# Cross-attention on one core: buffers that no store holds, a transfer moved behind x1, product 7 copied later

## The chip, the cores and the metric

The kernel runs on one core of one Trainium2 chip. The metric is the time of one execution in device microseconds. The engines are named as in the profile: PE is the matmul engine, PEld its weight loads, DVE the vector engine, ACT the scalar engine, POOL the engine GpSimd, SP the engine that issues plain transfers. All data are float32.

## The reference

For each of 8 batches, with x1 and x2 of 512 channels by 1024 positions:

```
q = einsum('bcn,dc->bnd', x1, Wq) + bq        # d = 64
k = einsum('bcn,dc->bdn', x2, Wk) + bk
v = einsum('bcn,dc->bdn', x2, Wv) + bv
attn = softmax(einsum('bnd,bdm->bnm', q, k), axis=2)
out = einsum('bcm,bnm->bcn', v, attn) + x1
```

## The kernel before

The two large products of a batch are done in two stages: Y = x2 · attn (the "y" stage), and then out = Wv · Y (the "o" stage). The bias is added at the end, since each row of attn sums to one. Each stage is split two by two and done with seven products in place of eight (the Strassen-Winograd scheme): products 1, 2, 6, 7, 5, 3, 4. The sums of operands that this takes are S1 to S4 of the left and T1 to T4 of the right operand. In the "y" stage products 1, 2, 7, 5, 3 and 4 are split once more by the same scheme from batch 1 on (`multiply_seeded`, `multiply_onto`): seven inner products of two by two matmuls, whose partial state in one PSUM tile (`chain`) is copied out by ACT between them. An inner product that adds on to `chain` must wait for the copy that comes before it. Inner products run in the order 1, 7, 6, 2, 5, 4, 3, and a dictionary `hooks` names other work that is issued after one of them.

The results of the "y" stage are blocks 11, 12, 21, 22. A PSUM pair of banks `a` collects products 1, 6, 5, 3, and a pair `c` products 2, 7, 4. States in between are copied to buffers in SBUF, each with a tag; tiles of one tag share one buffer (`bufs=1`), and a later tile waits until all use of the earlier one is over, a store to DRAM included. The tags that matter here:

- `u1`: product 1's copied state (`copy_u1`, line 332), then a part of product 5's inner sums (`eI5u`, line 434), then product 7's copied state (`copy_7`, line 534), then the result's block 11 (`evict_o`, line 605), which x1 is added to and which is stored from there.
- `u6`: the copied state of product 6, in the "y" and in the "o" stage. Block 21 of the result is made in it, in place (line 609), and is stored from there.
- `yT1`: an operand sum of the "o" stage, and inner sums of products 7 and 1 of the "y" stage.
- `y12`: a part of product 7, then the operand T3 of the "o" stage.

Softmax is done column by column of the transposed scores, in two halves h of 512 queries. The maximum over the rows is folded on DVE (line 248) and reduced over the partitions on POOL (`highest`, line 258). The sum of the exponentials of half 0 is not folded on DVE from batch 1 of the next scores on: ACT copies the first of four tiles (`copy_first`, line 621), and three transfers on POOL's queue add the others to it (`add_tile`, line 618). Each of these must have landed before the next is issued. Then DVE adds the two halves of the tile (line 252, in `total`), POOL reduces (line 263), and the reciprocal takes a way through DRAM (lines 265 to 278).

x1 is added to the result by transfers that accumulate, also on POOL's queue: `add_x1` for block 21 (line 565) and line 615 for the other blocks. `add_11` (line 171) adds a block of x2 to S3 and S2 in the same way. Stores of the result are issued by SP (line 616).

The order of work on each engine is the order in which the program issues it (`manual_schedule`); each engine and each queue works in that order. `period` issues one batch's steps: `s` is the batch, `n` the next, `nn` and `nnn` those after it. In the last part of `period` the "o" stage of `s` runs while the scores and exponentials of `n` are prepared.

Of the kernel before, what the change touches and what calls it, by code (L numbers as in the profile page):

```python
# [15 lines left out]
def kernel(  # L16
# [278 lines left out]
    def exponential(s, h, i):  # L295
        e = s.e[h][:, :, i, :]
        nc.scalar.activation(e, e, AF.Exp)  # L297
# [10 lines left out]
    def open_t(s):  # L308
        for n in ("T1", "T2"):
            s.t[n] = sb.tile([P, MH, H], F32, tag=f"e{n}", name=f"e{n}_{s.b}")  # L310
        e0, e1 = s.e[0], s.e[1]
        s.t |= {"11": e0[:, 0], "12": e1[:, 0], "21": e0[:, 1], "22": e1[:, 1]}
        s.t["T3"] = s.t["12"]
# [17 lines left out]

    def copy_u1(s, j):
        if j == 0:
            s.tmp[1] = sb.tile([P, 2, H], F32, tag="u1", name=f"uy1_{s.b}")
        nc.scalar.copy(s.tmp[1][:, j, :], s.bank["a", j])  # L335

    def sum_e(s, *ks, of=(0, 2)):
# [196 lines left out]
    def copy_7(s, j):  # L534
        if j == 0:
            s.tmp[7] = sb.tile([P, 2, H], F32, tag="u1", name=f"uy7_{s.b}")
        nc.scalar.copy(s.tmp[7][:, j, :], s.bank["c", j])
# [29 lines left out]
    def evict_o(s, k):  # L567


        bank, add = RESULT[k] if k != "11" else ("p", None)  # L570
        r, h = int(k[0]) - 1, int(k[1]) - 1

        def bias(j):
            return bv_sb[:, 2 * r + j : 2 * r + j + 1]

        if s.b == B - 1 and k == "11":
            o = s.x[:, 0:2, ts(h, H)]
            for j in range(2):
                nc.vector.scalar_tensor_tensor(
                    o[:, j, :], s.bank[bank, j], bias(j), o[:, j, :], ALU.add, ALU.add  # L580
                )
                nc.sync.dma_start(out[s.b, ts(j, P), ts(h, H)], o[:, j, :])
            return
        if s.b == B - 1 and add is None:
            for j, n, engine in (
                (0, slice(0, H), nc.sync), (1, left, nc.scalar), (1, right, nc.sync)
            ):
                o = s.x[:, 2 * r + j, ts(h, H)][:, n]
                nc.vector.scalar_tensor_tensor(
                    o, s.bank[bank, j][:, n], bias(j), o, ALU.add, ALU.add  # L590
                )
                engine.dma_start(out[s.b, ts(2 * r + j, P), ts(h, H)][:, n], o)
            return
        if s.b == B - 1:
            o = s.x[:, 2 * r : 2 * r + 2, ts(h, H)]
            for j in range(2):
                nc.vector.scalar_tensor_tensor(
                    o[:, j, :], s.bank[bank, j], bias(j), o[:, j, :], ALU.add, ALU.add
                )
            for j in range(2):  # L600
                nc.vector.tensor_tensor(o[:, j, :], o[:, j, :], s.tmp[add][:, j, :], ALU.add)
                nc.sync.dma_start(out[s.b, ts(2 * r + j, P), ts(h, H)], o[:, j, :])
            return
        if add is None:
            o = sb.tile([P, 2, H], F32, tag="u1" if k == "11" else "r", name=f"r{k}_{s.b}")
            for j in range(2):
                nc.scalar.activation(o[:, j, :], s.bank[bank, j], AF.Identity, bias=bias(j))
        else:
            o = s.tmp[add]
            for j in range(2):  # L610
                nc.vector.scalar_tensor_tensor(
                    o[:, j, :], s.bank[bank, j], bias(j), o[:, j, :], ALU.add, ALU.add
                )
        if k != "21":
            nc.gpsimd.dma_start(o, block(s, k, x1), accum_op=ALU.add)
        nc.sync.dma_start(block(s, k, out), o)

    def add_tile(s, h, i):
        nc.gpsimd.dma_start(s.mx[h], s.e[h][:, :, i, :], accum_op=ALU.add)  # L619

    def copy_first(s, h):

        s.mx[h] = sb.tile([P, 2, H], F32, tag="fold", name=f"sum_{s.b}_{h}", bufs=2)
        nc.scalar.copy(s.mx[h], s.e[h][:, :, 0, :])  # L624
# [138 lines left out]
    def period(s, n, nn, nnn):  # L763
# [32 lines left out]
        def add_exponential(i):  # L796
            exponential(n, 0, i)
            add_tile(n, 0, i)

        open_t(s)  # L800
        if n is None:
            load_x(s, x1)
        if s.b == 0:
            first(1)
            head_second(s, n)
            sum_e(s, "T1", "T2")
            total(s, 0)
            load_a(n, "11")
            first(2)
            evict_y(s, "11")  # L810
            keys(n)
            load_x(nn, x1)
            sum_t4(s)
            sums(s, 1)
            shares(s, 0)
            sum_e(s, "T3")
            load_a(n, "21", "22")
            first(6)
            scores_0()
            inner_left(s, 4, s.a["22"], "a12")  # L820
            inner_right(s, 4, s.t["T4"], "eT2")
            inner_left(s, 3, s.a["S4"], "aI3")
            shares(s, 1)
            first(5)
            inner_right(s, 3, s.t["22"], "eT1")
            for i in range(MH):
                lower(n, 0, i)
            first(7)
            copy_7(s, 0)
            copy_7(s, 1)  # L830
            complete_3 = multiply_seeded(s, 3, "r")
            complete_3()
            evict_t3(s)
            evict_y(s, "22")
            scale_y(s, "11", "T3", "22")
        else:
            complete_1 = multiply_seeded(s, 1, "y11")
            sum_e(s, "T1", "T2")
            complete_1()
            for i in range(1, MH):  # L840
                fold(s, 1, i, "sum", ALU.add)
            total(s, 1)
            invert(s, 0)
            complete_2 = multiply_seeded(
                s, 2, "y22", {5: lambda: copy_u1(s, 0), 4: lambda: copy_u1(s, 1)}
            )
            if n:
                sum_t3(s, 0)
                sum_t3(s, 2)
            complete_2()  # L850
            evict_y(s, "11")
            if n is None:
                sum_e(s, "T3")
            sum_t4(s)
            first(6)
            inner_left(s, 7, s.a["S3"], "yT4")
            if five:
                inner_left(s, 5, s.a["S1"], "i2")
                inner_right(s, 5, s.t["T1"], "y21", "u1")
            sum_a(s, "S4")  # L860
            if n:
                evict_q = scores_0()
            spread(s, 0)
            shares(s, 1)
            inner_right(s, 7, s.t["T3"], "yT1", "yT2")
            inner_left(s, 3, s.a["S4"], "aI3")
            if five:
                multiply_5(s, {6: evict_q})
            else:
                first(5)  # L870
            inner_right(s, 3, s.t["22"], "eT1")
            if n:
                lower(n, 0, 0)
            complete_7 = multiply_seeded(s, 7, "y12")
            complete_7()
            evict_y(s, "22")
            if n:
                for i in range(1, MH):
                    lower(n, 0, i)
            else:  # L880
                inner_left(s, 4, s.a["22"], "a12")
                inner_right(s, 4, s.t["T4"], "eT2")

            hooks = {7: lambda: copy_7(s, 0), 2: lambda: copy_7(s, 1)}
            if n:
                hooks |= {6: lambda: exponential(n, 0, 0), 4: lambda: exponential(n, 0, 1)}
            complete_3 = multiply_seeded(s, 3, "r", hooks)
            complete_3()
            evict_t3(s)
        if n:  # L890
            if s.b:
                load_a(n, "11")
            begin_s1(n)
            scores_and(n, 1, 2, "a", nothing)
            if s.b == 0:
                exponential(n, 0, 0)
            else:
                copy_first(n, 0)
                add_tile(n, 0, 1)
            end_s1(n)  # L900
            if nn:
                next_keys()
# [13 lines left out]
        if s.b == 0:  # L916
            hooks = {6: lambda: exponential(n, 0, 1), 5: lambda: exponential(n, 0, 2)}
        elif n:
            hooks = {6: lambda: add_exponential(2), 5: lambda: exponential(n, 0, 3)}
        multiply_4(s, hooks)  # L920
        if late and n:
            negate(n, "S3")
# [7 lines left out]
        if late and n:  # L930
            for i in range(1, MH):
                fold(n, 1, i, "max", ALU.max)
            highest(n, 1)
            add_tile(n, 0, 3)
            add_11(n, "S3")
        second(1)
        if s.b == 0:
# [14 lines left out]
        second(2)  # L952
        evict_o(s, "11")
        if n:
            if s.b == 0:
                add_tile(n, 0, 3)
            inner_left(n, 1, n.a["11"], "i2")
        second(5)
        if n:
# [58 lines left out]
```

## Time and profile before

| | us |
|---|---|
| time, median of 3 runs | 689.28 |
| lowest and highest of the 3 | 687.08, 691.88 |
| time of the profiled execution | 690.05 |
| its span, from the first to the last instruction | 688.0 |
| PE busy in it | 674.7 |
| DVE busy | 614.7 |
| ACT busy | 336.5 |
| POOL busy | 218.5 |

The span is that of one execution, and the other 2.05 us of its time lie around it. Busy times are sums over the span; an engine's idle time matters only where another engine, or the end, waits for it. DMA transfers are told by their issue and by the time until they land; POOL's queue carried 54.60 MB and the queue of SP 75.64 MB. The mean granted clock of PE was 0.998 of full speed.

### The profile page before, as it was taken

The page shows a single profiled execution, that of the slowest core. Times are in us where ns is not written, and L with a number is a line of the kernel's source. Part 1 is how long each engine was busy: PE and PEld are TensorE (multiplying, and loading weights), DVE is VectorE, ACT ScalarE, POOL GpSimd, SP SyncE. Part 2 cuts the span into 40 slices and gives each one's busy share as a digit, 9 for nine tenths or more (in the row PEclk, how much of TensorE's full clock was granted, in tenths as well). Part 3 has the DMA queues.
Part 4 walks back from the last instruction along what each step waited for, and adds up shares of the span by engine and source line. Part 5 has one row for each costly group of instructions (what it writes and reads, how often), then busy time and mean ns, then how long its engine had stood idle before and what let it go on. Part 6 is the DMA issues. An engine that isn't in the chain of part 4 may idle for free.

```text
span 688.0 us, 7199 instructions
## 1 busy us (share of the span) xinstructions
PE 674.7 (98%) x2420; PEld 399.0 (58%) x2420; DVE 614.7 (89%) x763; ACT 336.5 (49%) x564; POOL 218.5 (32%) x182
## 2 busy tenths in 40 slices
PE   9999999999999999999999999989999999999997
PEld 5333554766556665657647485463854747555763
DVE  1999998899999999999899999987989979999784
ACT  2734365456455464463743556515475356553320
POOL 0124215260265312542144421534213460264000
PEclk9999999999999999999999999999999999999999
DMA  9666659976996949979499785898747982699403
GB/s 303 262 216 238 127 216 155 241 146 206 235 228 184 248 121 285 197 189 287 107 257 226 166 253 146 199 219 200 230 82 170 243 177 63 122 163 278 111 10 113
DMA packets 50772, 131.09 MB, mean 191 GB/s; under 512 B 5552, under 2 KB 7856, under 8 KB 50736
## 3 DMA queue, kind: packets, MB, share of 16 engines
q0 software_dynamic: 22464, 54.60, 44.0%
q1 hardware_dynamic: 27984, 75.64, 30.4%
q10 hardware_dynamic: 288, 0.39, 0.2%
q8 instruction: 19, 0.31, 0.2%
q14 instruction: 17, 0.14, 0.1%
HBM read 87.30 MB, written 16.81 MB: 151 GB/s over the span
## 4 chain that ended last, share of the span: by engine, by line
PE 70%; DMA 15%; DVE 6%; issue 5%; ACT 2%; POOL 2%; SPq 0%; DVEq 0%; POOLq 0%; ACTq 0%
PE ps_ya L380 11%; PE ps_yc L442 6%; PE ps_oa L380 6%; PE ps_ya L442 6%; PE ps_s L228 5%; DMA r<-in_x_dram 5%; DMA out_dram<-r 4%; DMA sum<-e 4%; PE ps_oc L380 4%; PE ps_k L181 3%; PE ps_q L181 3%; PE ps_i4chain L442 3%; PE ps_o L400 3%; PE ps_i3chain L442 3%; PE ps_i7chain L442 2%
## 5 line engine op out<-in xcount | busy, mean ns | idle before, releaser
L380 PE MATMUL ps_ya<-eT,aS 128*128 128x512 f32 x176 | 79.5, 606 | 5.6 <-ACT uy L335 5.6
L263 POOL PARTITION_ALL_REDUCE den<-sum x16 | 52.6, 3285 | 93.0 <-DVE few L271 52.4
L258 POOL PARTITION_ALL_REDUCE top<-max x16 | 37.0, 2315 | 131.6 <-DVE max L252 75.9
L293 DVE TENSOR_TENSOR e<-e,top 128x1024 f32<-128x1024 f32 x60 | 69.9, 1218 | 0.0
L297 ACT ACTIVATE e<-e 128x1024 f32<-128x1024 f32 x60 | 61.8, 1057 | 4.6 <-DVE e L293 3.9
L619 POOL DMA_DIRECT2D sum<-e x21 | 25.4, 1208 | 115.8 <-ACT sum L624 45.5
L380 PEld LDWEIGHTS ps_ya<-eT,aS 128*128 128x128 f32 x176 | 33.6, 193 | 47.8 <-issue 38.7
L380 PE MATMUL ps_oa<-yT,w_S 128*128 128x512 f32 x128 | 57.5, 592 | 0.0
L380 PE MATMUL ps_oc<-yT,w 128*128 128x512 f32 x128 | 57.4, 592 | 0.0
L237 ACT COPY e<-ps_s 128x1024 f32<-128x1024 f32 x46 | 45.6, 1031 | 9.1 <-PE ps_s L228 8.8
L228 PE MATMUL ps_s<-q,k 64*128 64x512 f32 x188 | 47.6, 608 | 0.9 <-ACT q L646 0.8
L380 PEld LDWEIGHTS ps_oc<-yT,w 128*128 128x128 f32 x128 | 24.3, 190 | 30.6 <-issue 28.9
L380 PEld LDWEIGHTS ps_oa<-yT,w_S 128*128 128x128 f32 x128 | 24.3, 190 | 30.6 <-issue 30.6
L248 DVE TENSOR_TENSOR max<-max,e 128x1024 f32<-128x1024 f32 x30 | 36.8, 1225 | 2.2
L391 ACT COPY uo<-ps_oa 128x512 f32<-128x512 f32 x32 | 18.7, 585 | 35.0 <-PE ps_oa L380 33.9
L391 ACT COPY uy<-ps_ya 128x512 f32<-128x512 f32 x24 | 13.9, 589 | 39.1 <-PE ps_ya L380 36.8
L228 PEld LDWEIGHTS ps_s<-q,k 64*128 64x128 f32 x188 | 17.0, 186 | 24.5 <-issue 17.5
L479 ACT COPY ps_ya<-ps_i1chain 128x256 f32<-128x256 f32 x28 | 10.0, 357 | 42.2 <-PE ps_i1chain L442 38.7
L547 DVE TENSOR_TENSOR y<-y,den 128x1024 f32<-128x1024 f32 x24 | 29.3, 1221 | 0.3
L418 DVE TENSOR_TENSOR aI<-a 128x256 f32<-128x256 f32 x58 | 29.0, 541 | 0.0
L380 PE MATMUL ps_oa<-y,w_S 128*128 128x512 f32 (+1 forms) x68 | 28.8, 567 | 0.0
L400 PE MATMUL ps_o<-y,w 128*128 128x512 f32 x64 | 28.8, 592 | 0.0
(201 smaller groups left out, 1549.6 us busy)
## 6 DMA issues: line engine op xcount, KB each, us to landing
x_in_x_dram<-in_x_dram SPq DMA_DIRECT2D x60, 512.0 KB, 6.9
a<-in_x2T_dram SPq DMA_DIRECT2D x32, 512.0 KB, 9.8
sum<-e POOLq DMA_DIRECT2D x21, 512.0 KB, 6.0
aS<-in_x2T_dram POOLq DMA_DIRECT2D x14, 512.0 KB, 8.8
uo<-in_x_dram POOLq DMA_DIRECT2D x14, 512.0 KB, 10.3
r<-in_x_dram POOLq DMA_DIRECT2D x14, 512.0 KB, 12.3
out_dram<-r SPq DMA_DIRECT2D x14, 512.0 KB, 6.2
out_dram<-uo SPq DMA_DIRECT2D x14, 512.0 KB, 4.6
```

The source lines that it names most:

```text
L181: nc.tensor.matmul(ps[r, :], w_sb[:, c, :], s.x[:, c, ts(h, H)], start=(c == 0), stop=(c == CT - 1),)
L228: nc.tensor.matmul(ps[g], s.k[r, ts(i, P)], s.q[r, ts(h, H)], start=True, stop=True)
L237: nc.scalar.copy(e[:, :, i, :], whole)
L248: nc.vector.tensor_tensor(f, e[:, :, 0, :] if i == 1 else f, e[:, :, i, :], op)
L258: nc.gpsimd.partition_all_reduce(s.top[h], s.mx[h][:, 0, :], P, ReduceOp.max)
L263: nc.gpsimd.partition_all_reduce(s.den[h], s.mx[h][:, 0, :], P, ReduceOp.add)
L293: nc.vector.tensor_tensor(e, e, top, ALU.subtract)
L297: nc.scalar.activation(e, e, AF.Exp)
L380: nc.tensor.matmul(ps[:, n], left[ka][:, k, ts(j, P)], right[kb][:, k, n], start=opens and k == 0, stop=i in (2, 3, 4) and k == n_k - 1, s ...
L391: nc.scalar.copy(s.tmp[i][:, j, :], ps)
L400: nc.tensor.matmul(ps, w["11"][:, k, ts(j, P)], s.y["11"][:, k, :], start=k == 0, stop=False, skip_group_check=True)
L442: nc.tensor.matmul(ps, s.inner[i][ka][:, k, :], s.inner[i, "t"][kb][:, k, :], start=opens and k == 0, stop=z in (2, 3, 4) and k == MH // 2 ...
```

## The change

Four things are done.

1. Product 1's copied state goes to the buffer `yT1` in place of `u1`. The result's block 21 goes to `y12`; before, it was made in place in `u6`. The number of instructions is the same.
2. The third of the transfers that sum half 0 is issued after `add_11` of S3, after `add_x1` of block 21, and after x1's transfer for block 11 (in `evict_o`). In batch 0 it was there already.
3. Product 7's state is copied after the second and the fifth inner product of product 3 in place of the seventh and the second.
4. In batch 6, where there is a next batch and none after it, the copy and the first transfer of half 0's sum are issued in product 4, after its seventh inner product, and no longer before it.

```diff
     def copy_u1(s, j):
         if j == 0:
-            s.tmp[1] = sb.tile([P, 2, H], F32, tag="u1", name=f"uy1_{s.b}")
+            s.tmp[1] = sb.tile([P, 2, H], F32, tag="yT1", name=f"uy1_{s.b}")
         nc.scalar.copy(s.tmp[1][:, j, :], s.bank["a", j])
...
         else:
-            o = s.tmp[add]
+            u = s.tmp[add]
+            o = sb.tile([P, 2, H], F32, tag="y12", name=f"o{k}_{s.b}") if k == "21" else u
             for j in range(2):
                 nc.vector.scalar_tensor_tensor(
-                    o[:, j, :], s.bank[bank, j], bias(j), o[:, j, :], ALU.add, ALU.add
+                    o[:, j, :], s.bank[bank, j], bias(j), u[:, j, :], ALU.add, ALU.add
                 )
...
+        def first_sum():
+            copy_first(n, 0)
+            add_tile(n, 0, 1)
...
-            hooks = {7: lambda: copy_7(s, 0), 2: lambda: copy_7(s, 1)}
+            hooks = {2: lambda: copy_7(s, 0), 5: lambda: copy_7(s, 1)}
...
             if s.b == 0:
                 exponential(n, 0, 0)
-            else:
-                copy_first(n, 0)
-                add_tile(n, 0, 1)
+            elif nn:
+                first_sum()
             end_s1(n)
...
         elif n:
             hooks = {6: lambda: add_exponential(2), 5: lambda: exponential(n, 0, 3)}
+            if nn is None:
+                hooks[7] = first_sum
         multiply_4(s, hooks)
...
             highest(n, 1)
-            add_tile(n, 0, 3)
             add_11(n, "S3")
         second(1)
...
         evict_o(s, "11")
         if n:
-            if s.b == 0:
-                add_tile(n, 0, 3)
+            add_tile(n, 0, 3)
             inner_left(n, 1, n.a["11"], "i2")
```

## The prediction

> **What bounds the kernel now.** I read the page first, then the list of waits of the matmul engine, then the timeline around its longest wait.
>
> ```profile
> span 688.0 us, 7199 instructions
> PE 674.7 (98%) x2420; PEld 399.0 (58%) x2420; DVE 614.7 (89%) x763; ACT 336.5 (49%) x564; POOL 218.5 (32%) x182
> ```
>
> PE is busy for 674.7 of 688.0 us, so nothing that runs beside it is worth anything: only PE's own idle time, 13.3 us with head and tail, and any slow matmuls can be won. Who ends that idle time (waiter, who was waited for: us, times, longest):
>
> ```profile
> PE ps_ya L380 <- ACT uy L335: 5.6, 3, 3.8
> PE ps_i3chain L442 <- ACT ps_ya L479: 1.0, 1, 1.0
> PE ps_warm L691 <- DVE warm L688: 1.0, 1, 1.0
> PE ps_s L228 <- ACT q L646: 0.8, 1, 0.8
> PE ps_ya L380 <- ACT e L288: 0.3, 1, 0.3
> PE ps_i4third L442 <- ACT e L237: 0.3, 1, 0.3
> ```
>
> The first line is `copy_u1` (line 335): three times the matmuls of product 6 stand until product 1's state has been copied. The second is one wait in product 3. The rest is the head and 0.3 us in batch 6. The timeline tells why the copy is late (start, duration, what; in brackets the idle time before it and what ended it):
>
> ```profile
> 430.96 1.19 POOL L619 DMA_DIRECT2D sum<-e  x1 [9.07 <-ACT ps_oa L404]
> 435.36 1.89 POOL L258 PARTITION_ALL_REDUCE top<-max  x1 [3.21 <-DVE max L252]
> 441.67 1.20 POOL L619 DMA_DIRECT2D sum<-e  x1 [4.42 <-ACT e L297]
> 442.97 2.04 POOL L565 DMA_DIRECT2D uo<-in_x_dram  x1
> 443.73 2.50 POOL L615 DMA_DIRECT2D r<-in_x_dram  x1
> ...
> 450.73 0.68 DVE L252 TENSOR_TENSOR sum<-sum 128x512 f32<-128x512 f32 x1
> 453.43 1.41 DVE L611 SCALAR_TENSOR_TENSOR uo<-ps_oc,bv_sb,uo 128x512 f32<-128x512 f32 x2 [2.02 <-DMA uo<-in_x_dram]
> ...
> 455.94 0.40 SPq L616 DMA_DIRECT2D out_dram<-r  x1
> ...
> 458.40 1.23 DVE L306 TENSOR_TENSOR eT<-eT,e 128x1024 f32<-128x1024 f32 x1
> ...
> 465.34 0.58 ACT L335 COPY uy<-ps_ya 128x512 f32<-128x512 f32 x1 [4.52 <-DMA out_dram<-r]
> ...
> 465.97 8.83 PE L380 MATMUL ps_ya<-eT,aS 128*128 128x512 f32 x16 [3.83 <-ACT uy L335]
> ```
>
> The third transfer of half 0's sum (441.67) stood on POOL for the second to land, and x1 for block 11 (443.73) stood behind it. That x1 lands as SP issues the store, 455.94; the store reads buffer u1, which the copy on ACT must overwrite, so ACT waits for it until 465.34 and PE until 465.97. PE then takes 8.83 us for 16 instructions that take 7.13 us at 379.89. The windows say why (columns: us, busy time and instructions of PE, PEld, DVE, ACT, POOL, granted clock, DMA share, GB/s):
>
> ```profile
> 466.00:471.00 5.00, 5.00 (x8) 2.19 (x9) 4.63 (x11) 4.48 (x6) 4.70 (x6) 0.66 0.61 206
> ```
>
> After the 3.83 us pause the granted clock is low for some 3.4 us.
>
> **The change part by part.** *The copied state in yT1.* No instruction is added. The copy now waits for the last reader of yT1, the matmuls of product 1's own inner sums, over by 455.3 here, instead of the store. In this place the next thing to end is T2 for product 6 at 458.40+1.23 = 459.63, while PE reaches product 6 at 462.1, so no second wait stands close behind. Gone: the 5.6 us of line 335 (0.20 at 379.89, 3.83 at 465.97, 1.57 at 628.05) and 8.83-7.13 = 1.70 us of slow matmuls. The wait on the store passes to the next user of u1, DVE's line 434 for product 5's inner sums at 472.46; the store had landed by 465.3, so 7 us are to spare, and a store still later would cost DVE the excess.
>
> The Trainium skill ("TensorE: Matmul & The Clock Gate", "What's actually happening") has the clock fall only after an idle window of about 3.4 us that runs freely, so a pause like this one costs clock in some runs and none in others. The 1.57 us pause here kept a clock of 1.00, which fits. By the page the 1.70 us might be missing from a median run, and the time would be 683.4 us in place of the one below; I keep the row.
>
> *Block 21 in y12.* DVE's two additions (1.41 us for both) write another buffer. u6 is then free when they end (about 454.8) and not when the store lands. ACT's copy of product 6 waited for that store once, 2.3 us, with PE not stopped: worth nothing by itself, but without it a 2.3 us wait could show once PE runs earlier. y12's readers, the matmuls of the second stage's product 7, are over some 3 us before, and its next writer, a copy in product 7, comes more than 20 us after the store's issue (at 490 against 465.34).
>
> *The third transfer behind x1.* On POOL it passes three issues from batch 1 on: `add_11` of S3, x1 for block 21, x1 for block 11. These three no longer wait for the second transfer; around 441 they would issue from 437.25, when the top reduction ends, and x1 of block 11 land about 6 us earlier. The price is that `sum` lands last of the four. Transfers of this queue land one after the other (issue to landing 5.5 us for the first, then about 2.5 to 3 us each), so the four end about where x1 of block 11 ended before, 0.4 to 0.6 us earlier where POOL had waited. Against the start of DVE's line 252:
>
> - batches 1 to 6, old landing (the store's issue, line 616): 204.87, 287.22, 369.04, 455.94, 538.50, 616.79;
> - DVE reaches line 252 at 204.28, 286.28, 368.27, 450.73, 538.51, 616.13.
>
> That makes a new DVE wait of 0 to 0.7 us each, and about 1.2 us at 450.73 (four landings of some 2.6 us after the second's 441.1 give 451.9), where the old 2.02 us wait for x1 of block 21 goes. Behind it on DVE are block 21, T1 and T2, and product 6 waits for T2. T2 ends 2.3 to 3.7 us before PE gets there (294.03 against 297.69 in an undisturbed stretch), so PE pays nothing. Later DVE has about 0.44 us before product 7's completion and 0.75 us before product 3's. Bounds: 0 and six times 1 us; I take 0, since batch 0 has just this order already, and a longer wait:
>
> ```profile
> 123.81 0.69 DVE L252 TENSOR_TENSOR sum<-sum 128x512 f32<-128x512 f32 x1 [3.13 <-DMA sum<-e]
> 161.96 0.58 ACT L537 COPY uy<-ps_yc 128x512 f32<-128x512 f32 x1 [1.45 <-DVE y L556]
> 162.87 1.13 PE L442 MATMUL ps_i3chain<-eI3eT,aI 128*128 128x256 f32 x4 [1.04 <-ACT ps_ya L479]
> ```
>
> A wait of 3.13 us cost PE 1.04 us, 39 us later, because `copy_7` on ACT stood for DVE and the copy that frees `chain` stood behind it.
>
> *Product 7 copied later.* Both copies (0.58 us) move two inner products back, behind that copy (0.38 us) and an exponential (1.06 us). The `chain` copy comes right after its matmuls, so the 1.04 us go. What stands behind `copy_7` now is the copy for inner product 3, whose matmuls come two inner products (2 x 0.86 us) after those that waited, so the tolerance for a late DVE grows by 1.7 us. The 0.3 us of batch 6 stay; its first transfer, put off into product 4, takes a 1.09 us copy of ACT from before that product to its middle: -0.3 to +0.5, taken as 0.
>
> *Sum.* 5.6 + 1.7 + 1.04 = 8.3 us. The profiled execution took 690.05 us (688.0 of span, 2.05 around it), so 681.7 us. The median shown is 689.28 us and the lowest 687.08; I read their 4.8 us of spread as these stalls being longer or shorter, over one floor. I set no other offset.
>
> **Rivals.** *Part comes back* (20%). The pauses go, but DVE, 89% busy, becomes the bound after 466, where PE comes 5.5 us earlier. For it: DVE's idle time there is 2.02+0.53+0.91+3.03 = 6.5 us, and 1.2 us of new wait leave it level. Against it: the other stretches run level without a stop of PE. At 2 to 3 us back: 684 us. The missing clock loss ends in the same place.
>
> *The wait only moves* (6%). Something else holds ACT's copy or product 6, such as its own left operand or DVE's completion of product 1. Against it: both were through about 2 to 4 us before PE. Only the 1.04 us would go: 689 us.
>
> *Slower: the sum lands late in every batch* (7%). The place is DVE's line 252. The slack before product 6 is 3.65 us; what is above stops PE, six times. The net is a loss from 3.65+8.3/6 = 5.0 us. For it: one x1 transfer took 17.2 us to land; issued at about 275.2 that is 292.4, a wait of 6.1 us, and 681.7 + 6 x 2.45 = 696.4 us. Against it: the longest `sum` took 11.5 us, at four in a row.
>
> **How the numbers follow.** The forecast has 67%: 681.7 us, alone 680.3 to 683.5. A measurement of this kernel can tell about 1% from no change, here below 682.4 or above 696.2 us. The forecast lies close to the first bound: some 50 of its 67 fall below, and 2 of the part that comes back, so faster 0.52. Slower takes half of its rival and a little for what I overlooked: 0.06. The rest, 0.42, is within 1%. The range reaches up to the part that comes back: 680.3 to 686.5.
>
> **What would show it.** Right: no wait of PE on line 335 and none of `ps_i3chain`, a clock of 1.00 from 7 us to the end, no ACT wait on `out_dram<-r`, DVE line 252 waiting 0 to 1.5 us for `sum<-e` in batches 1 to 6, PE busy 673 us in a span near 680. Wrong: PE waits on `eT` or on lines 485 and 306, a DVE wait at line 252 above 3 us, or line 434 waiting for a store.

## The result, and the profile after

| | before | after |
|---|---|---|
| median, us | 690.28 (4 runs, 687.08 to 691.88) | 682.42 (4 runs, 681.23 to 682.56) |
| profiled execution: time, span | 690.05, 688.0 | 682.56, 680.8 |
| PE busy in it | 674.7 | 672.1 |

The ratio is 0.9888, with a 95% interval of 0.9848 to 0.9928: 1.1% faster. The forecast was 681.7 us.

From the page after:

```profile
span 680.8 us, 7209 instructions
PE 672.1 (99%) x2420; PEld 397.9 (58%) x2420; DVE 615.2 (90%) x763; ACT 336.9 (49%) x564; POOL 218.5 (32%) x182
```

PE is busy 2.6 us less with the same 2420 instructions. Most of it is one stretch that ran at half the clock before. PE's waits after (waiter, who was waited for: us, times, longest):

```profile
PE ps_warm L692 <- DVE warm L689: 1.0, 1, 1.0
PE ps_sa L228 <- DVE yT L542: 0.9, 1, 0.9
PE ps_k L181 <- DMA x_in_x_dram<-in_x_dram: 0.8, 2, 0.6
PE ps_s L228 <- ACT q L647: 0.8, 1, 0.8
PE ps_q L643 <- DMA x_head<-in_x_dram: 0.7, 1, 0.7
PE ps_ya L380 <- ACT e L288: 0.3, 1, 0.3
PE ps_i4third L442 <- ACT e L237: 0.3, 1, 0.3
```

The wait for `copy_u1` is gone, and so is the one of `ps_i3chain`. In their place stands one new wait, for line 542 (`evict_t3`), 0.9 us. The waits for `ps_k` and `ps_q` are the first loads from DRAM. The timeline around the place of the longest pause, after:

```profile
437.64 0.92 POOL L171 DMA_DIRECT2D a<-in_x2T_dram  x1
438.20 1.59 POOL L565 DMA_DIRECT2D uo<-in_x_dram  x1
438.91 2.08 POOL L616 DMA_DIRECT2D r<-in_x_dram  x1
442.42 1.18 POOL L620 DMA_DIRECT2D sum<-e  x1 [1.42 <-DMA sum<-e]
...
449.59 0.40 SPq L617 DMA_DIRECT2D out_dram<-r  x1
452.11 0.69 DVE L252 TENSOR_TENSOR sum<-sum 128x512 f32<-128x512 f32 x1 [0.77 <-DMA sum<-e]
...
458.65 1.23 DVE L306 TENSOR_TENSOR eT<-eT,e 128x1024 f32<-128x1024 f32 x1
...
461.25 0.60 ACT L335 COPY uy<-ps_ya 128x512 f32<-128x512 f32 x1
...
462.51 7.03 PE L380 MATMUL ps_ya<-eT,aS 128*128 128x512 f32 x16
```

x1 of block 11 (`r`) is issued right behind the reduction, and its store at 449.59 in place of 455.94. The third transfer is issued last of the four, and DVE waits 0.77 us for it at line 252. The copy has no idle time in front of it in brackets, and the 16 matmuls of product 6 take 7.03 us in place of 8.83. The granted clock (the column behind POOL's busy time) in the same window as before:

```profile
466.00:471.00 5.00, 5.00 (x17) 2.10 (x17) 4.86 (x11) 2.48 (x5) 4.70 (x6) 1.00 0.04 1
```

It is 1.00 where it was 0.66. PE works on 17 matmuls there, the end of product 6 and the first scores, where it was 8 of product 6 alone.

### The profile page after: what moved, and what is told of

Read it like the earlier page. It is cut to its first block, busy times and chain, and to the rows that moved or that the text cites. A ratio compares the mean times of both kernels' runs of the same rounds, so it can differ in the third digit from the quotient of the medians.

```text
span 680.8 us, 7209 instructions
## 1 busy us (share of the span) xinstructions
PE 672.1 (99%) x2420; PEld 397.9 (58%) x2420; DVE 615.2 (90%) x763; ACT 336.9 (49%) x564; POOL 218.5 (32%) x182
## 4 chain that ended last, share of the span: by engine, by line
PE 84%; DVE 6%; DMA 5%; issue 2%; ACT 1%; SPq 1%; POOL 1%; DVEq 0%; POOLq 0%; ACTq 0%
PE ps_ya L380 11%; PE ps_oa L380 11%; PE ps_yc L442 8%; PE ps_oc L380 7%; PE ps_ya L442 6%; PE ps_s L228 5%; PE ps_o L400 4%; PE ps_o L380 4%; PE ps_k L181 3%; PE ps_q L181 3%; PE ps_i4chain L442 3%; PE ps_i3chain L442 3%; PE ps_i7chain L442 2%; PE ps_i1chain L442 2%; PE ps_i2chain L442 2%
## 5 line engine op out<-in xcount | busy, mean ns | idle before, releaser
L380 PE MATMUL ps_ya<-eT,aS 128*128 128x512 f32 x176 | 77.5, 594 | 0.0
L620 POOL DMA_DIRECT2D sum<-e x21 | 32.1, 1530 | 108.7 <-ACT sum L625 42.0
```

The costliest lines, as they stand in the source:

```text
L380: nc.tensor.matmul(ps[:, n], left[ka][:, k, ts(j, P)], right[kb][:, k, n], start=opens and k == 0, stop=i in (2, 3, 4) and k == n_k - 1, s ...
```

## Experiments

Two theories for the main gain stand against each other: the copy had to leave the buffer that the store holds, or the store had to be earlier. The first two runs do one part each, on the kernel before. One measure is used throughout: PE runs the same 2420 matmuls in every version, so when the same matmul starts in two traces tells how far PE is ahead or behind at that place. An idle time can set it back by more than its own length, since the matmuls behind a pause start further apart.

**The buffers alone.**

```diff
-            s.tmp[1] = sb.tile([P, 2, H], F32, tag="u1", name=f"uy1_{s.b}")
+            s.tmp[1] = sb.tile([P, 2, H], F32, tag="yT1", name=f"uy1_{s.b}")
...
+            o = sb.tile([P, 2, H], F32, tag="y12", name=f"o{k}_{s.b}") if k == "21" else u
```

> The kernel before with the first part alone: product 1's state in yT1, block 21 in y12. My theory (the buffer held by the store is the whole cause of the three pauses): no wait of PE on line 335, granted clock 1.00 after the head, although x1 of block 11 lands as late as before (about 11 to 12 us after its issue, its store landing after product 2's end at least in one batch). No DVE wait at line 252 from batch 1 on. One PE wait of about 1.0 us in product 3 stays. Time 682 to 683 us. Rival (the transfer's place is what counts): PE still waits 2 us or more in all at product 6, for T2 or the left operand, and the time is 685 us or more.

Measured: 681.54 us (4 runs, 681.28 to 682.0) beside 689.71 before, ratio 0.989 (0.9866 to 0.9914). Its timeline:

```profile
455.50 0.40 SPq L617 DMA_DIRECT2D out_dram<-r  x1
...
460.31 0.59 ACT L335 COPY uy<-ps_ya 128x512 f32<-128x512 f32 x1
...
461.57 7.03 PE L380 MATMUL ps_ya<-eT,aS 128*128 128x512 f32 x16
```

The store is issued as late as before (455.50; it lands 9.3 us later in the trace, at 464.8), and PE is in product 6 before that. So the buffer alone takes away the whole pause. The wait of `ps_i3chain` is there with 1.0 us and DVE does not wait at line 252 from batch 1 on, both as expected; the time is 0.5 us under the expected range.

**The transfer's place alone.**

```diff
             highest(n, 1)
-            add_tile(n, 0, 3)
             add_11(n, "S3")
...
-            if s.b == 0:
-                add_tile(n, 0, 3)
+            add_tile(n, 0, 3)
```

> The kernel before with the second part alone: the third transfer of half 0's sum behind x1 of block 11, product 1's state still in u1. My theory: x1 of block 11 lands 2 us earlier in each batch and some 6 us earlier where POOL had waited, so the store is over when the copy comes, or up to 0.5 us later: PE waits on line 335 for under 1 us in all, no loss of clock, DVE waits 0.1 to 1.5 us at line 252 in each of six batches; 682.5 to 684 us. The two parts then remove the same time twice over and must not be added. Rival (only the buffer helps): pauses of 3 us or more stay, 686 us or more.

Measured: 682.26 us (681.45 to 682.68), ratio 0.9902 (0.9873 to 0.993). PE has no wait on line 335. Its timeline:

```profile
441.01 1.18 POOL L619 DMA_DIRECT2D sum<-e  x1 [1.46 <-DMA sum<-e]
...
448.23 0.40 SPq L616 DMA_DIRECT2D out_dram<-r  x1
450.75 0.69 DVE L252 TENSOR_TENSOR sum<-sum 128x512 f32<-128x512 f32 x1 [0.86 <-DMA sum<-e]
...
459.81 0.59 ACT L335 COPY uy<-ps_ya 128x512 f32<-128x512 f32 x1
...
461.06 7.03 PE L380 MATMUL ps_ya<-eT,aS 128*128 128x512 f32 x16
```

Here the copy still uses u1, but the store issued at 448.23 lands 10.0 us later, at 458.3, 1.5 us ahead of the copy. In another batch ACT still stood 0.5 us for this store, and PE did not feel it. The time is 0.2 us under the expected range. Each of the two parts removes the same pauses by itself. They must not be added, and done together the second is a reserve.

**yT1 alone, block 21 left in u6.** The first line of the diff above.

> The kernel before with product 1's state in yT1 and nothing else; block 21 stays in u6. Forecast: block 21's buffer is worth nothing by itself, so this equals the two buffers together, 681.5 us within 0.7 us, with no PE wait on line 335. Rival: without the second buffer ACT's copy of product 6 waits for the store of block 21 (2.3 us once before) and PE, which is earlier now, shows 0.5 to 2.5 us of it in front of the scores or product 5: 682.5 us or more.

Measured: 682.33 us (681.94 to 683.25), ratio 0.9906 (0.988 to 0.9932). PE waits 0.2 us for ACT's copy of product 6, once, in the last batch: that copy goes to u6 and stood 4.46 us for the store of block 21. By the starts of the same matmuls in this trace and in that of the two buffers, the wait set PE back by 0.4 us. So block 21's buffer is worth 0.4 us here, and not nothing as the forecast had it. The medians lie 0.8 us apart, just outside the 0.7 us given, and the two ranges overlap by 0.06 us; the other 0.4 us can't be told from the spread of the runs.

**The old order of product 7's copies**, in the kernel after.

```diff
-            hooks = {2: lambda: copy_7(s, 0), 5: lambda: copy_7(s, 1)}
+            hooks = {7: lambda: copy_7(s, 0), 2: lambda: copy_7(s, 1)}
```

> The changed kernel with product 7 copied after inner products 7 and 2 as before. My theory, from the profile after: DVE is late in batch 1, and PE pays about 0.9 us for that at whichever step comes to need it first; so the 0.9 us wait for line 542 goes and a wait of about 1 us in product 3 is back: same time within 0.3 us, 682.4 us. In the other batches nothing. Rival (the forecast's step: the later copies win 1.04 us): 1 us more, 683.5 us, with the wait at line 542 kept or other waits of PE in product 3 in batches 2 to 6.

Measured: 681.82 us (681.55 to 682.22). PE's waits show what came of it:

```profile
PE ps_i3chain L442 <- ACT ps_ya L479: 1.1, 1, 1.1
```

The wait for line 542 is gone, and the one in product 3 is back. Moving the copies moved PE's wait and took nothing off it. The time is 0.6 us below the forecast of this run; the two profiled spans are 1.0 us apart, and 0.8 us of that had arisen by batch 0's keys, where the first loads from DRAM are waited for.

**Batch 0's third transfer ahead of the x1 transfers.** If both waits have one cause, DVE's late start at line 252 after batch 0, an earlier landing there should remove either.

```diff
             add_tile(n, 0, 2)
+            add_tile(n, 0, 3)
             value_sums("S3", "S4")
...
-            add_tile(n, 0, 3)
+            if s.b:
+                add_tile(n, 0, 3)
```

> The changed kernel with batch 0's third transfer issued right behind the second, ahead of the x1 transfers. Theory (DVE's wait of 3.2 us at line 252 after batch 0 is what PE pays 0.9 us for in batch 1): it lands some 5.5 us after the second, DVE waits under 0.5 us there, PE waits neither for line 542 nor in product 3 of batch 1: 0.9 to 1.4 us less, 681.2 us. Rival (DVE is late in batch 1 by its own work): PE's 0.9 us stay, 682.4 us.

Measured: 680.71 us (679.8 to 680.96), ratio 0.9878 (0.9852 to 0.9904). PE's waits in full:

```profile
PE ps_warm L692 <- DVE warm L689: 1.0, 1, 1.0
PE ps_s L228 <- ACT q L647: 0.8, 1, 0.8
PE ps_ya L380 <- ACT e L288: 0.3, 1, 0.3
PE ps_i4third L442 <- ACT e L237: 0.3, 1, 0.3
```

DVE does not wait at line 252 after batch 0, and between the head and batch 6 PE waits for nothing. That shows the cause of the 0.9 us. By the starts of the same matmuls in both traces, PE was 1.3 us ahead of the kernel after by the end of batch 0's keys (the first loads, which vary from run to run), and gained 1.4 us more in batch 1. So the wait of 0.9 us cost more than the idle time that the list shows.

**The same two kernels once more, on one chip.**

> The changed kernel again, on one chip with the version that follows it. Theory (its head varies with the first loads by 1 us or so, the rest is fixed): 681.5 to 682.5 us, PE's wait for line 542 in batch 1 of about 0.9 us again, clock 1.00, no wait on line 335. Rival (the 0.9 us were chance): no such wait, 681 us.

> The changed kernel with batch 0's third transfer right behind the second, again. Theory: PE does not wait for line 542; 1.2 us less than the changed kernel beside it (680.5 to 681.2 us). Rival (the 680.7 us of the first run were a fast head alone): within 0.4 us of the changed kernel.

Measured: the changed kernel 682.24 us (6 runs, 681.13 to 682.76), with a PE wait of 0.8 us for line 542 again; the version with batch 0's transfer early 680.47 us (5 runs, 680.07 to 680.85), without it. The two ranges do not meet. The medians lie 1.8 us apart where 1.2 was expected. In this pair of traces the changed kernel is 0.1 us ahead behind the first loads, and falls 1.4 us back in batch 1; nothing else differs by 0.1 us. Against the kernel before (688.62 there) the ratios are 0.991 (0.989 to 0.9929) and 0.9885 (0.9867 to 0.9903). This version beats both kernels.

**yT1 and batch 0's early transfer on the kernel before, nothing else.**

> The kernel before with product 1's state in yT1 and batch 0's third transfer right behind the second: the two edits that should be enough. Theory: no PE wait on line 335, none in product 3 of batch 1, no loss of clock: PE waits only in the head and 0.3 us in batch 6, 680.5 us, 1.0 us less than the buffers alone and 1 to 2 less than the changed kernel. Rival (the copies of product 7 or the other edits are needed too): 682 us or more.

Measured: 681.74 us (681.11 to 682.37), ratio 0.9898 (0.9868 to 0.9929). PE has no wait on line 335 and none in product 3, as expected, but the time missed by 1.2 us. A wait of 0.3 us for ACT at the scores of batch 1 is new, and 0.1 us for the copy of product 6 in the last batch shows. Both go back to one buffer:

```profile
139.71 1.07 ACT L391 COPY uy<-ps_ya 128x512 f32<-128x512 f32 x2 [4.10 <-DMA out_dram<-uo]
141.75 1.13 PE L228 MATMUL ps_s<-q,k 64*128 64x512 f32 x4 [0.31 <-ACT e L237]
625.60 1.14 ACT L391 COPY uy<-ps_ya 128x512 f32<-128x512 f32 x2 [4.43 <-DMA out_dram<-uo]
```

Line 391 copies product 6 to u6, which the store of block 21 still holds. ACT stood for that store four times, 10.9 us in all, and never in the runs that move block 21 to y12. By the starts of the same matmuls, against the trace with batch 0's transfer early (680.37 us), the two waits set PE back by 0.6 and 0.4 us, and product 4 of batch 6, without the transfer put off, by 0.1 us. That is about the miss. The worth of the two edits in this kernel is read from the traces; they were not added to it one by one.

**The transfer later still**: the kernel after, with the third transfer of batches 1 to 6 behind the addition to S2, so that DVE waits for it longer.

```diff
-            add_tile(n, 0, 3)
+            if s.b == 0:
+                add_tile(n, 0, 3)
...
             add_11(n, "S2")
+            if s.b:
+                add_tile(n, 0, 3)
```

> The changed kernel with the third transfer moved one place further in batches 1 to 6, behind the addition to S2. This puts a number on the slack that made the moved transfer free. It should land some 6 us after DVE could begin line 252 (in the profile after, the addition to S2 lands at 208.8 and the next transfer of this queue some 2.6 us later, against 205.1). By the slack of 3.65 us from the prediction PE waits for T2 about 2.7 us in each of six batches: 682.4 + 16 = 698 to 699 us. With a second payment in product 3 or at the scores, as batch 1 shows for a late DVE (0.9 us), 704 us. Rival (DVE's delay is absorbed elsewhere, or there is no such slack): no more than 2 us lost in all, under 685 us; or the whole 6 us are paid each time, 718 us.

Measured: 697.65 us (697.14 to 698.27), ratio 1.0127 (1.0101 to 1.0153). The size is close to the expected one, but by luck: DVE waited only 3.4 to 5.4 us at line 252 where some 6 were expected, and by the slack of 3.65 us those six waits would have cost 5.8 us in all, not 15.2. PE's longest waits:

```profile
PE ps_sa L228 <- DVE yT L542: 5.7, 5, 1.3
PE ps_i2chain L442 <- ACT ps_yc L479: 1.8, 1, 1.8
PE ps_s L228 <- ACT e L237: 1.1, 4, 0.3
```

There is no wait for T2 among them. The timeline of batch 2:

```profile
293.41 0.69 DVE L252 TENSOR_TENSOR sum<-sum 128x512 f32<-128x512 f32 x1 [4.75 <-DMA sum<-e]
...
299.83 7.03 PE L380 MATMUL ps_ya<-eT,aS 128*128 128x512 f32 x16
...
336.04 1.29 DVE L542 TENSOR_TENSOR yT<-ps_ya,uy 128x512 f32<-128x512 f32 x2
...
336.78 1.29 PE L228 MATMUL ps_sa<-q,k 64*128 64x512 f32 x3 [1.26 <-DVE yT L542]
```

DVE stands 4.75 us at 293.41, and PE starts product 6 at 299.83 on time. It pays 43 us later, when the scores of half 1 need the pair of banks `a` that line 542 has still to read. That is also where the kernel after pays its 0.9 us. PE's idle time, span less busy time, is 7.7 us longer than after, half of the 15.4 us between the spans; the other half stands as busy time, 679.8 us in place of 672.1, with the clock at 1.00. Each pause of 1.26 us at these scores set PE back by 2.1 us.

**The kernel before, profiled once more.**

> The kernel before, profiled once more. My theory (its spread of 4.8 us is the length of the pauses over one floor): PE's waits on line 335 and the loss of clock differ from those of the first profile, and the span less these is the same within 0.7 us: 688.0 - 5.6 - 1.7 = 680.7 us. Rival (the spread is elsewhere): the same pauses with another span, or a remainder off by 1.5 us or more.

Measured: 690.40 us, span 688.4. PE waits 5.3 us on line 335, 3.5 of them in one pause, again before product 6 at 466, and the granted clock falls again:

```profile
466.00:472.00 6.00, 5.62 (x9) 2.41 (x10) 5.23 (x12) 5.08 (x8) 5.70 (x7) 0.72 0.61 203
```

With about 1.8 us for the clock the remainder is 688.4 - 5.3 - 1.8 = 681.3 us, against 688.0 - 5.6 - 1.8 = 680.6 us in the first profile: within the 0.7 us expected, and both close to the span after. The before runs spread over 686.34 to 691.44 us on one chip, those after over 681.13 to 682.76. So most of the spread goes away with the pauses. But the two profiles of before have nearly the same pauses and lie in the upper part of the range, so they say little on the spread, and no timeline shows what a run near 687 us did. The mean granted clock of the runs tells more: of 27 runs of the kernel before for which it is on record, the five below 687.3 us had 1.000, and the others, all above 688.1, had 0.994 to 0.998 (the profiled execution, with its one stretch at half clock, 0.998). A mean clock of 0.994 over 688 us is a loss of some (1 - 0.994) x 688 = 4.1 us, an estimate. By it the spread is for the most part lost clock, and less the length of the pauses, as the prediction had read it. The five kept their clock and still took 4 to 5 us longer than the runs after; presumably they paused too, but that was not seen.

## Why the prediction was right, and where it was not

- **The pauses** (5.6 us). Right: gone, in the place and by the mechanism named. That each of two parts would do it alone was not said; the sum charged it once, so the number held. The term was too small: by the starts of the same matmuls the pauses of 0.20 and 1.57 us set PE back by 0.48 and 1.84 us, 0.27 us more each, and that of 3.83 us, with its lost clock of some 1.7, by 5.79. That is 0.8 us over the idle times.
- **The slow matmuls** (1.70 us). Right, and slightly undersized: 8.83 against 7.03 us is 1.80. In both profiles of before, the clock fell behind the long pause (3.83 and 3.52 us), 1.18 and 1.39 us after PE had started again, and stayed at 0.5 for 3.41 us. Behind the pauses of 1.57 us, and of 1.85 us in the run with the transfer later still, it stayed at 1.00. The Trainium skill ("TensorE: Matmul & The Clock Gate", "What's actually happening") has the clock fall after at least one idle window of about 3.4 us that runs freely. These traces fit that in the lengths, but not plainly in the place: the 3.41 us just before each fall hold more than 1 us of matmuls, and whether the fall comes late or a window need not be idle throughout can't be told here.
- **Product 7 copied later** (1.04 us). This is the step that failed. The `ps_i3chain` wait went as worked out, and the tolerance at that place grew. But DVE was as late as before, and the next to need it, the scores' use of the banks `a` after line 542, took it back: PE stood there for 0.89 us. From the timeline after:

```profile
163.05 0.57 ACT L537 COPY uy<-ps_yc 128x512 f32<-128x512 f32 x1
163.82 0.59 ACT L537 COPY uy<-ps_yc 128x512 f32<-128x512 f32 x1
166.60 0.69 DVE L485 TENSOR_TENSOR ps_ya<-ps_ya,v 128x512 f32<-128x512 f32 x1
167.20 1.28 DVE L542 TENSOR_TENSOR yT<-ps_ya,uy 128x512 f32<-128x512 f32 x2
167.94 1.29 PE L228 MATMUL ps_sa<-q,k 64*128 64x512 f32 x3 [0.89 <-DVE yT L542]
```

  The copies end long before DVE comes to line 485: it was DVE, not ACT, that was late. I asked what the copy stands in front of and not what DVE's own lateness stops next. By the starts of the same matmuls the wait in product 3 had set PE back by 1.4 us before, and the wait at line 542 set it back by 1.5 us after: nothing of the term was left. With it at 0 the sum would be 7.3 us and the time 682.8 us, against 682.42.
- **The third transfer last of four.** x1 of block 11 was stored 6.35 us earlier where about 6 were worked out. DVE's waits were 1.47, 0.15, 0.22, 0.77, 0.46 and 1.10 us; 0 to 0.7 was given, and 1.2 for the fourth. Two of the forecasts were too small by up to 0.8 us, and none of these waits reached PE. For the fourth the working slips: four landings of 2.6 us behind 441.1 end at 451.5, not 451.9, which makes a wait of 0.8 us, the one measured.
- **The price of the slower rival** (3.65 us of slack before product 6, then PE pays). Wrong in the slack, the place and the price; that the run with the transfer later still came near the expected time was luck, as said there. With waits up to 5.4 us product 6 did not wait for T2. One reason can be read in the timeline and was not tried by itself: T2 is made in halves, and product 6 reads the second half only from its fifth matmul on, 1.7 us after its start. Behind the longest wait product 6 started at 635.82, the second half was ready at 637.31, and the fifth matmul began at 637.53. The real limit lay later, at the scores, and nearer: 3.1 to 3.2 us of wait after batch 0 already made PE stand for 0.9 us.
- **Block 21 in y12.** Right that it is worth nothing as long as PE stands elsewhere, and that the wait for the store could show once PE runs earlier: left in u6 it cost 0.4 us in one run and 1.0 us in another, as the experiments show.
- **The first transfer of batch 6 put off** (taken as 0). From product 4's first to its fifth inner product PE took 4.46 us before and 4.23 after: 0.23 us won, of which 0.1 us is left by the end of the product, inside the bounds.
- **What was left out.** The head. In the profile after, PE stood 0.7 and 0.8 us for the first loads, and by batch 0's keys it was 0.7 us later than in the profile before; the version with batch 0's transfer early had none of it. A term of up to 1 us either way was missing from the sum, though not from the range.

By the starts of the same matmuls, the three pauses with the lost clock account for 8.1 us, and the transfer put off in batch 6 for 0.1; the head takes 0.7 back, and small shifts some 0.3: 7.2 us, the difference of the two spans. So the forecast sum of 8.3 us is near in part by luck: the pauses cost 0.8 us more than their idle time, product 7's 1.04 us did not come, and the head cost 0.7.

## What to carry to other kernels

A tile that a store reads from holds its buffer until the store has landed, so put into that buffer nothing that the busiest engine waits for; a free buffer of the same size costs no instruction. When two edits aim at one wait, price them together, since each may remove all of it. When a wait is removed by giving an engine more time at one step, follow the late engine to its next customer: a lateness that nothing shortens is paid at the next place.

## What the runs showed of the hardware

A pause of PE of 3.83 or 3.52 us cost about half as much again: in both profiles of before the granted clock stood at 0.5 for 3.41 us, from 1.2 and 1.4 us after PE had started again. Shorter pauses, too, set PE back by more than the idle time shown: by 0.27 us more before product 6, by 0.4 in product 3, and by 0.3 to 0.9 at the scores.

In the profile before, a transfer of 512 KB that accumulates, issued while nothing else of POOL's queue was under way, took 5.1 to 5.6 us to land in ten of 14 cases and up to 10.7 in the others. One behind others landed 2.2 to 6.9 us after the one ahead of it, 51 of 82 within 3.1 us, among them reads of x1, of x2 and of exponentials. Its place in the queue set its landing more than the moment of its issue: x1 for the block issued at 447.65 took 17.2 us.
